# The extra block of a graph network's quantile layer: 16-bit words collected on ScalarE, trees for both neighbours apart, candidates in halves

## The chip, the cores and the metric

The kernel runs on one core of a Trainium2 chip. The metric is the time of one execution on the device in microseconds (us). Engines are named as in the profile: PE is TensorE, PEld its weight load, DVE is VectorE, ACT is ScalarE, POOL is GpSimd, SP is SyncE, which only issues transfers.

## The reference

Four graph layers in sequence over 16 graphs of 1024 nodes with 64 channels; each layer is `x = x + layer(relu(layernorm(x)), adj)`. Only layer 0 bears on the change. For each node it takes the neighbours that are left after a rule has dropped some, sorts their values in each channel, and mixes three quantiles:

```python
vals = jnp.where(nd[..., None], x[:, None, :, :], jnp.inf)
s = jnp.sort(vals, axis=2)
nv = nd.sum(2)
for tau, w in zip((0.25, 0.5, 0.75), (0.25, 0.5, 0.25)):
    pos = tau * jnp.maximum(nv - 1, 0)
    lo, hi = floor(pos), ceil(pos)
    agg = agg + w * (v_lo + (pos - lo) * (v_hi - v_lo))   # entries lo and hi of s
y = relu((x + agg) @ W1 + b1) @ W2 + b2
```

Layers 1 to 3 multiply by the adjacency, with gates, with a small MLP, and with a softmax of attention.

## The kernel before

The 16 graphs are worked on in eight pairs. For a pair, all 1024 values of every channel are sorted once (`sort_pair`); the sorted order is cut into words of 11 values. A product of the neighbour matrix with codes of rank (`wt`, line 975) gives for each node, channel and word a number that packs how many neighbours lie up to there and which of the word's values are neighbours. From these numbers the wanted place is found by maxima over the words (a tree), the bits are decoded (`places`, 28 small VectorE operations), and the value is picked from candidates that TensorE forms from signs and a table of the sorted values (`pick`: five predicated copies; `add_to`: the weighted sum).

`select` does this for one graph in groups of two row tiles of 128 nodes, with windows: only those words are looked at in which a quantile normally lies. Nodes whose quantile lies outside its window are flagged. At the end of `select`, before the values of its last group, `compact` collects the flagged nodes of the graph, at most 64: it gathers their rows of the neighbour matrix and makes all 56 words for them, in seven pieces of eight words (`PIECES`, 512 columns each; line 1288 multiplies, line 1292 evicts), and writes them to DRAM (`x_d`). Graph 0 of the pair has partitions 0 to 63, graph 1 has 64 to 127. It also writes a selection table (`sel_d`) that takes the results back to the nodes.

After both graphs `extras` handles the collected nodes of the pair, 128 rows at once and all words: it loads `x_d` (line 1308), clears and loads the two tables `tab` (lines 1312, 1314), and for each of the three quantiles k evicts the words as 16-bit integers with the quantile's place as a bias (line 1326), transposes them (1333), takes two signs (1336, for the lower and the upper neighbour of the quantile), adds 2048 for the upper neighbour (1340) and runs the tree over both at once (1004 and 1008, in `maxima`), with two outputs z and odd (1346, 1347). Then `places` for all six, and six times: 64 small products into one candidate tile of four PSUM banks (1357), five predicated copies (1065) and the weighted sum (1072, 1074). Last, for each graph of the pair, the selection table is loaded (1365), multiplied (1368) and the flagged nodes of `agg` are overwritten (1369).

Then come the four layers of both graphs (`layers`), which need `agg`. Beside `extras` and `layers`, in the first seven pairs, run the next pair's `neighbours` (scan of line 879, squares of 908 and 909, blocks of 929; transposed copies of the adjacency, lines 885 to 888, which ScalarE evicts and writes out) and the rest of its sort (lines 804 to 814); the forward half of the sort (772 to 776) also runs beside `select`. The last pair has no next one.

The order of instructions on each engine is not the order of the text: a planner orders them by estimated costs, earlier text first among those ready. Each engine then works through its own list in that order. Buffers are tiles of pools; with one buffer of a name, the next tile of that name waits for the last reader of the one before. The memory of `extras` (pool `xs`) is that of `select` before and of `layers` after.

Of the kernel before, what the change touches and what calls it, by code (L numbers as in the profile page):

```python
# [14 lines left out]
I16 = mybir.dt.int16  # L15
# [27 lines left out]
def gnn_stack(ctx, tc, x, adj, nodemask, w, out):  # L43
# [25 lines left out]
    ones_b = const.tile([P, N], BF16, name="ones_b")  # L69
# [92 lines left out]
    x_d = dram.tile([P, NW * C], F32, name="x_d")  # L162
# [292 lines left out]
    def general(gw):  # L455
# [47 lines left out]
        with tc.For_i(0, B, 1) as b:  # L503
            with ExitStack() as per_batch:
# [13 lines left out]
                with (  # L518
# [5 lines left out]
                    notrem = nb1.tile([P, NT, N], BF16, name="notrem")  # L524
                    for t in range(NT):
# [11 lines left out]
                        nc.vector.tensor_tensor_scan(cum, ones_b, ni, 0.0, op0=ALU.mult, op1=ALU.add)  # L537
# [522 lines left out]
    def pick(cand, masks):  # L1060

        v = cand.rearrange("p q (d l) -> p q d l", l=24)
        for (dst, frm, n), mk in zip(PICKS, masks):
            mk = mk.rearrange("p (q d o) -> p q d o", d=4, o=1)
            nc.vector.copy_predicated(
                v[:, :, :, dst : dst + n], mk.to_broadcast([P, NQ, 4, n]), v[:, :, :, frm : frm + n]
            )
        return v[:, :, :, 11]
# [158 lines left out]
    def compact(b, i, wt, row10, out_of, kept, cp, cpp):  # L1227
# [40 lines left out]
        nc.scalar.copy(vx[mine, :], pv[mine, :9])  # L1268
        rows = cp.tile([P, N], F8, name="rows")
# [11 lines left out]
        for u in range(0, len(PIECES), 2):  # L1281
            two = PIECES[u : u + 2]
            n = len(two) * 512
            xr = cp.tile([P, 1024], F32, name="xr")
            for e, g in enumerate(two):
                pw = bank()
                for j in range(NT):
                    nc.tensor.matmul(  # L1288
                        pw, ndx[:, j, :], wt[g][:, j].rearrange("p w c -> p (w c)"),
                        start=(j == 0), stop=(j == NT - 1),  # L1290
                    )
                nc.scalar.copy(xr[mine, e * 512 : (e + 1) * 512], pw[mine])
            nc.sync.dma_start(x_d[mine, two[0] * 512 : two[0] * 512 + n], xr[mine, :n])
# [8 lines left out]
    def extras(pr, kept, aggs, xs, xp):  # L1302

        vx = kept["vx"]
        comb = xs.tile([P, NW * C], F32, name="comb_x")
        for u in range(0, len(PIECES), 2):
            at = slice(PIECES[u] * 512, (PIECES[u] + len(PIECES[u : u + 2])) * 512)
            nc.scalar.dma_start(comb[:, at], x_d[:, at])
        tabs = []
        for i in range(2):  # L1310
            tab = xs.tile([4 * NH, NQ, 4, 48], F16, name=f"tab{i}")
            nc.vector.memset(tab, 0.0)
# [6 lines left out]
        qx = xs.tile([P, 3], F32, name="qx")  # L1319
        nc.vector.tensor_scalar(qx, vx[:, :3], -2048.0, -2048.0, op0=ALU.mult, op1=ALU.add)  # L1320
        signs = []
        z = xs.tile([P, 1, 6, C], U16, name="z_x")
        odd = xs.tile([P, 1, 6, C], U16, name="odd_x")
        for k in range(3):
            y = xs.tile([P, 2, 2 * NQ, 4 * NH], I16, name="y_x", bufs=2)
            nc.scalar.activation(
                y[:, 0].rearrange("p r (h d) -> p r h d", d=4),
                comb.rearrange("p (h r d) -> p r h d", r=2 * NQ, d=4),
                AF.Identity, bias=qx[:, k : k + 1], scale=1.0,
            )  # L1330
            pt = xp.tile([P, 2, 512], F32, name="tr").bitcast(BF16).rearrange("p e (q n) -> p (e q) n", n=P)
            for q in range(NQ):
                nc.tensor.transpose(pt[: 4 * NH, q, :], y[:, 0, q, :].bitcast(BF16), ident_b)
# [6 lines left out]
            nc.vector.tensor_scalar_add(y[:, 1], y[:, 0], 2048.0)  # L1340
            yu = y.bitcast(U16)
            maxima(yu, NH)
            ev, od = yu[:, :, :NQ, :4], yu[:, :, NQ:, :4]
            zs = z[:, 0, 2 * k : 2 * k + 2, :].rearrange("p s (q d) -> p s q d", d=4)
# [373 lines left out]
```

## Time and profile before

| what | value |
|---|---|
| median of 3 runs | 5775.26 us (5774.35 to 5782.18) |
| profiled execution, own time | 5786.15 us |
| its span | 5784.4 us |
| busy: DVE / PE / ACT / PEld / POOL | 5034.9 / 4378.1 / 3789.4 / 2731.3 / 169.8 us |
| transfers | 551.45 MB, 519811 packets, mean 95 GB/s |
| collection's products, L1288 | 896, 379 ns each (median) |
| collection's copies, L1292 | 112, 580 ns each |
| extra block's evictions, L1326 | 24, 3281 ns each (median) |
| candidates' products, L1357 | 3072, 281 ns each (median) |
| first pair: extra block / layers | 684 to 792 / 792 to 982 us |
| last pair: extra block / layers | 5542 to 5619 / 5619 to 5784 us |

The busy times are of one profiled execution. A product's 281 ns is its length in a pipeline: 64 of them take 2.79 us in the last pair. In the same way ScalarE's and VectorE's instructions overlap a little with the one behind; a row of "743.4, 712" means that the group kept the engine busy 743.4 us in all and that one instruction lasted 712 ns.

### The profile page before, as it was taken

To read this page: it belongs to the slowest core of one execution; us is meant where nothing else is said; L and a number is where in the kernel's file an instruction comes from. 1 tells how busy PE (TensorE), PEld (TensorE's weight loads), DVE (VectorE), ACT (ScalarE), POOL (GpSimd) and SP (SyncE) were. 2 spreads that over 40 slices of the span, in tenths; PEclk is the share of its full clock that TensorE was granted. 3 is DMA by queue.
4 is the path that set the end of the run, shared out by engine and by line. 5 is a ranking of instruction groups with operands and counts; after the bars stand their busy time and mean duration, and the time that the engine had idled before them with its cause. 6 is when DMAs were issued, how large, how long until landed. Compare 5 with 4: busy or idle time off the path is not lost.

```text
span 5784.4 us, 114212 instructions
## 1 busy us (share of the span) xinstructions
PE 4378.1 (76%) x45010; PEld 2731.3 (47%) x45010; DVE 5034.9 (87%) x13175; ACT 3789.4 (66%) x5739; POOL 169.8 (3%) x292
## 2 busy tenths in 40 slices
PE   1488677896878958788588885788767886779956
PEld 1355443554435544455434554355543554535642
DVE  9899888998889987999879998899888998888755
ACT  2587657775586855867558666686657866477835
POOL 3000000000000000000000000000000000000000
PEclk5699878997789977899688996899878997789967
DMA  3401264013631047210562115611255012630030
GB/s 128 127 23 45 86 205 133 29 38 113 220 96 35 28 133 237 62 40 23 166 211 55 41 53 167 203 32 40 82 175 172 26 40 90 215 110 18 10 100 5
DMA packets 519811, 551.45 MB, mean 95 GB/s; under 512 B 263296, under 2 KB 413056, under 8 KB 519264
## 3 DMA queue, kind: packets, MB, share of 16 engines
q1 hardware_dynamic: 376864, 459.65, 25.5%
q10 hardware_dynamic: 140064, 81.84, 4.6%
q8 instruction: 355, 5.82, 0.4%
q0 software_dynamic: 2336, 2.57, 0.2%
q14 instruction: 192, 1.57, 0.1%
HBM read 360.17 MB, written 183.76 MB: 94 GB/s over the span
## 4 chain that ended last, share of the span: by engine, by line
PE 40%; DVE 24%; ACT 23%; DMA 9%; issue 3%; POOL 0%; SPq 0%; ACTq 0%; DVEq 0%; POOLq 0%
PE comb L1097 13%; ACT sign L1152 8%; PE cand L1197 6%; PE bank L1462 5%; DVE y L1168 4%; PE comb L1288 3%; ACT y L1105 3%; DMA adjT<-a_d 2%; DVE cum L879 2%; DMA a_d<-at 2%; DVE wt L975 2%; DVE cand L1205 2%; PE pk L929 2%; ACT nat L1128 1%; PE bank L1446 1%
## 5 line engine op out<-in xcount | busy, mean ns | idle before, releaser
L1097 PE MATMUL comb<-wt,ndT 128*128 128x512 fp8e5 x6144 | 1439.2, 386 | 144.4 <-ACT sign L1152 111.8
L1105 ACT ACTIVATE y<-comb,qb 128x512 int16<-128x512 f32 x1152 | 743.4, 712 | 505.3 <-PE comb L1097 504.2
L1097 PEld LDWEIGHTS <-ndT 128*128 128x128 fp8e5 x6144 | 591.1, 99 | 864.7 <-issue 231.6
L1152 ACT ACTIVATE sign<-comb,lower 128x1024 fp8e5<-128x1024 int16 (+1 forms) x640 | 694.5, 1085 | 0.0
L1152 ACT ACTIVATE sign<-comb,half 128x1024 fp8e5<-128x1024 int16 (+1 forms) x640 | 689.1, 1077 | 0.0
L1197 PE MATMUL cand<-vtab,sign 128*128 128x48 f16 (+1 forms) x18432 | 663.1, 191 | 23.1 <-DVE agg L1074 16.2
L1168 DVE TENSOR_TENSOR y<-y 128x512 uint16<-128x512 uint16 (+5 forms) x896 | 669.4, 789 | 10.8 <-PE comb L1150 10.0
L1197 PEld LDWEIGHTS <-sign 128*128 128x128 fp8e5 x18432 | 637.6, 96 | 82.0 <-issue 21.2
L1205 DVE COPY_PREDICATED cand<-w_f,cand 128x256 f32<-128x256 uint16 (+1 forms) x1536 | 531.9, 378 | 86.1 <-PE cand L1197 83.7
L887 ACT COPY at<-pk 128x512 f32<-128x512 f32 x256 | 147.3, 586 | 372.7 <-PE pk L885 199.8
L1150 PE MATMUL comb<-ident_b,y 128*128 128x128 bf16 x4608 | 307.2, 218 | 101.9 <-ACT sign L1152 70.8
L929 PE MATMUL pk<-minus_b,rem 128*128 128x128 bf16 x1024 | 231.9, 251 | 178.8 <-ACT rem L910 178.8
L1150 PEld LDWEIGHTS <-y 128*128 128x128 bf16 x4608 | 284.9, 97 | 127.1 <-issue 126.9
L929 PE MATMUL pk<-ident_b,ni 128*128 128x128 bf16 x1024 | 229.1, 247 | 110.4 <-ACT ndT L935 60.7
L879 DVE TENSOR_TENSOR_SCAN cum<-ni 128x1024 f16<-128x1024 fp8e5 x128 | 292.4, 2285 | 15.5 <-POOL ni L875 15.5
L885 PE MATMUL pk<-ident,a 128*128 128x128 f32 x1024 | 192.1, 330 | 149.9 <-DMA a<-in_adj_dram 100.1
L1462 PE MATMUL bank<-att,hs 128*64 128x512 f32 x512 | 191.1, 857 | 122.0 <-ACT hs L1578 122.0
L1462 PE MATMUL bank<-adjT,nd 128*64 128x512 f32 x896 | 256.2, 642 | 29.9 <-DMA adjT<-a_d 29.6
L975 DVE TENSOR_SCALAR wt<-node 128x2048 uint8<-128x2048 f16 x224 | 262.5, 1220 | 18.4 <-PE comb L1288 18.1
L775 DVE TENSOR_TENSOR s<-s 128x512 f32<-128x512 f32 (+1 forms) x440 | 276.0, 627 | 0.0
L776 DVE TENSOR_TENSOR s<-s 128x512 f32<-128x512 f32 (+1 forms) x440 | 275.1, 625 | 0.0
L1163 DVE TENSOR_SCALAR y<-y 128x4608 int16<-128x4608 int16 x128 | 173.5, 1355 | 90.7 <-ACT y L1105 89.3
(381 smaller groups left out, 8355.7 us busy)
## 6 DMA issues: line engine op xcount, KB each, us to landing
adjT<-a_d SPq DMA_DIRECT2D x336, 512.0 KB
a<-in_adj_dram SPq DMA_DIRECT2D x128, 512.0 KB
a_d<-at ACTq DMA_DIRECT2D x256, 256.0 KB
m_d<-swapped SPq DMA_DIRECT2D x104, 512.0 KB
swapped<-m_d SPq DMA_DIRECT2D x104, 512.0 KB
n_d<-nat SPq DMA_DIRECT2D x128, 128.0 KB
x_d<-xr SPq DMA_DIRECT2D x48, 256.0 KB
comb_x<-x_d ACTq DMA_DIRECT2D x24, 512.0 KB
```

The source lines that it names most:

```text
L775: nc.vector.tensor_tensor(to_lo, lo, hi, op=ALU.max)
L879: nc.vector.tensor_tensor_scan(cum[:, t - t0, :], ni[:, t, :], wide[:, t, pad - 1 : pad - 1 + N], 0.0, op0=ALU.add, op1=ALU.add)
L929: nc.tensor.matmul(pk[:, n % 4, :], lhs, rhs, start=(n % 4 == 0 and m == 0), stop=(m == len(terms) - 1 and last),)
L975: nc.vector.tensor_scalar(wt[g][:, :, k : k + 4, :].bitcast(U8), node, 4.0 * (25 + CODE * (8 * g + k)), 4.0 * 26, op0=ALU.add, op1=ALU.min,)
L1097: nc.tensor.matmul(pw, ndT[:, j, t * P : (t + 1) * P], wt[1 + g8][:, j].rearrange("p w c -> p (w c)"), start=(j == 0), stop=(j == NT - 1),)
L1105: nc.scalar.activation(y[:, 0, chunks, at : at + 8 * d_].rearrange("p q (w d) -> p q w d", d=d_), pw.rearrange("p (w q d) -> p q w d", w=8 ...
L1150: nc.tensor.transpose(pt[:, q - q0, :], y[:, 0, q, :].bitcast(BF16), ident_b)
L1152: nc.scalar.activation(signs[tl][s][:, q0:q1, :], pt.bitcast(I16), AF.Sign, bias=before[s], scale=-1.0, saturate=False,)
L1168: nc.vector.tensor_tensor(v[:, :, :, :n], v[:, :, :, :n], v[:, :, :, n : 2 * n], op=ALU.max)
L1197: nc.tensor.matmul(cand[:, e, at : at + 12 * d_].rearrange("p (d l) -> p d l", l=12), signs[tl][sec][:, chunk, :], tab[:, q, :, half_ * 12 ...
L1205: nc.vector.copy_predicated(v[:, :, :, dst : dst + k], mk.to_broadcast([P, 2, C // 2, k]), v[:, :, :, frm : frm + k])
L1462: nc.tensor.matmul(po[to : to + C, :], lhs, rhs[:, f * HALF : (f + 1) * HALF], start=(j == 0), stop=(j == NT - 1))
```

## The change

The words of the collected nodes no longer go to DRAM as 32-bit numbers and through ScalarE again in `extras`. `compact` evicts each piece three times, once for each quantile's bias, as 16-bit integers, into a tile with two buffers, and writes each piece to DRAM by itself. An eviction writes its output in order and reads the product in steps of four columns. `extras` loads the 16-bit words of all three quantiles with 12 transfers into one tile `y_x` with room for both neighbours, and transposes from it with words 32 elements apart.

The tables are cleared by GpSimd. One addition makes the upper neighbour's words of all three quantiles; the trees run once for the upper and once for the lower neighbour, over all three quantiles at a time, first over the pieces and then inside a piece. The upper neighbour's tree does not touch the words that the transposes read. The candidates come in halves of 8 chunks, in three tiles of two PSUM banks that the transposes and the last products use too. Both selection tables are loaded at once, from ScalarE's queue, into the memory of `y_x` when the trees are done with it. A constant of ones is made smaller to leave room; the general path that it served (not run here) gets its own.

```diff
-    x_d = dram.tile([P, NW * C], F32, name="x_d")
+    x_d = dram.tile([P, 7, 3, 512], I16, name="x_d")
...
     compact:
+        qx = cp.tile([P, 3], F32, name="qx")
+        nc.vector.tensor_scalar(qx[mine], pv[mine, :3], -2048.0, -2048.0, op0=ALU.mult, op1=ALU.add)
...
-        for u in range(0, len(PIECES), 2):
-            two = PIECES[u : u + 2]
-            xr = cp.tile([P, 1024], F32, name="xr")
...
-                nc.scalar.copy(xr[mine, e * 512 : (e + 1) * 512], pw[mine])
-            nc.sync.dma_start(x_d[mine, two[0] * 512 : two[0] * 512 + n], xr[mine, :n])
+        for g in PIECES:
+            xr = cp.tile([P, 3, 512], I16, name="xr", bufs=2)
+            pw = bank()
...
+            for k in range(3):
+                nc.scalar.activation(
+                    xr[mine, k].rearrange("p (h d r) -> p h d r", h=4, d=4),
+                    pw[mine].rearrange("p (h r d) -> p h d r", r=2 * NQ, d=4),
+                    AF.Identity, bias=qx[mine, k : k + 1], scale=1.0,
+                )
+            nc.sync.dma_start(x_d[mine, g], xr[mine])
...
     extras:
-        comb = xs.tile([P, NW * C], F32, name="comb_x")
-            nc.scalar.dma_start(comb[:, at], x_d[:, at])
+        y = xs.tile([P, 2, 3, 7, 512], I16, name="y_x")
+        for g in (1, 3, 5, 0):
+            for k in range(3):
+                here = slice(g, g + (2 if g else 1))
+                nc.scalar.dma_start(y[:, 0, k, here], x_d[:, here, k])
...
-            nc.vector.memset(tab, 0.0)
+            nc.gpsimd.memset(tab, 0.0)
...
         for k in range(3):
-            y = xs.tile([P, 2, 2 * NQ, 4 * NH], I16, name="y_x", bufs=2)
-            nc.scalar.activation(
-                y[:, 0].rearrange("p r (h d) -> p r h d", d=4),
-                comb.rearrange("p (h r d) -> p r h d", r=2 * NQ, d=4),
-                AF.Identity, bias=qx[:, k : k + 1], scale=1.0,
-            )
-            pt = xp.tile([P, 2, 512], F32, name="tr")
+            pt = xp.tile([P, 1024], F32, name="two", bufs=3)
+            by_word = y[:, 0, k].rearrange("p g (w r) -> p r (g w)", w=16)
             for q in range(NQ):
-                nc.tensor.transpose(pt[: 4 * NH, q, :], y[:, 0, q, :].bitcast(BF16), ident_b)
+                nc.tensor.transpose(pt[: 4 * NH, q, :], by_word[:, q].bitcast(BF16), ident_b)
...
-            nc.vector.tensor_scalar_add(y[:, 1], y[:, 0], 2048.0)
-            maxima(yu, NH)
+        nc.vector.tensor_scalar_add(y[:, 1], y[:, 0], 2048.0)
+        for s in (1, 0):
+            yu = y[:, s].bitcast(U16)
+            for n, m in ((3, 4), (2, 2), (1, 1)):
+                nc.vector.tensor_tensor(yu[:, :, :n], yu[:, :, :n], yu[:, :, m : m + n], op=ALU.max)
+            yw = yu[:, :, 0]
+            for n in (256, 128):
+                nc.vector.tensor_tensor(yw[..., :n], yw[..., :n], yw[..., n : 2 * n], op=ALU.max)
...
+        sel_t = xs.tile([P, 2, 3, 7, 512], I16, name="y_x")
+        for i in range(2):
+            nc.scalar.dma_start(sel_t[:, i], sel_d[i])
...
         for s in range(6):
-            cand = xp.tile([P, NQ, P], F32, name="cand")
-            for q in range(NQ):
+            for q0 in range(0, NQ, 8):
+                cand = xp.tile([P, 1024], F32, name="two", bufs=3)
+                for q in range(8):
...
-            v = pick(cand[:, :, :96], [mk[:, 0, s, :] for mk in (odd, *marks)])
+                here = slice(q0 * 4, (q0 + 8) * 4)
+                v = pick(cand[:, :, :96], [mk[:, 0, s, here] for mk in (odd, *marks)])
...
         for i in range(2):
-            sel_t = xs.tile([P, NT, P], F32, name="sel_t")
-            nc.sync.dma_start(sel_t, sel_d[i])
-            ps = xp.tile([P, 2, 512], F32, name="tr")
+            ps = xp.tile([P, 1024], F32, name="two", bufs=3)
```

## The prediction

> **What bounds the kernel now.** I read the page's busy times first, then its chain, then the windows of one pair and of the last pair, the chain of waits in the last pair's extra block, and the rows of the lines that change.
>
> ```profile
> span 5784.4 us, 114212 instructions
> PE 4378.1 (76%) x45010; PEld 2731.3 (47%) x45010; DVE 5034.9 (87%) x13175; ACT 3789.4 (66%) x5739; POOL 169.8 (3%) x292
> PE 40%; DVE 24%; ACT 23%; DMA 9%; issue 3%; POOL 0%; SPq 0%; ACTq 0%; DVEq 0%; POOLq 0%
> ```
>
> VectorE is the fullest engine, but the chain that ends last is on PE more often: the kernel is a relay of stages, and a stage must be read by itself. In the windows (PE, PEld, DVE, ACT, POOL busy, then granted clock, DMA share and GB/s):
>
> ```profile
> 684.00:700.00 16.00, 1.19 (x10) 0.92 (x10) 9.97 (x20) 4.25 (x2) 1.76 (x4) 0.50 0.82 246
> 684.00:792.00 108.00, 53.65 (x784) 46.31 (x784) 97.09 (x232) 68.46 (x86) 7.01 (x12) 0.67 0.50 153
> 792.00:982.00 190.00, 149.05 (x735) 70.92 (x735) 153.29 (x467) 119.98 (x168) 4.67 (x9) 0.79 0.61 194
> 5542.00:5612.00 70.00, 26.35 (x448) 24.56 (x448) 42.80 (x94) 21.10 (x9) 0.32 (x2) 0.50 0.33 117
> 5619.00:5784.00 165.00, 112.27 (x407) 50.65 (x407) 82.04 (x269) 79.08 (x107) 2.88 (x4) 0.72 0.02 4
> ```
>
> 684 to 792 is the first pair's extra block, 792 to 982 its four layers; the last two rows are the same two stages of the last pair, where nothing of a next pair runs beside them. In the first seven pairs the block is nearly full on VectorE (97 of 108 us), but only some 47 us of that is its own: the rest is the next pair's sort and neighbours. In the last pair the block is bare (42.8 of 70 us), and its chain shows what it waits for:
>
> ```profile
> 5542.38 1.34 DVE tab L1312
> 5543.99 1.34 DVE tab L1312
> 5545.38 3.29 ACT y_x L1326
> ...
> 5579.52 2.79 PE cand L1357 x64
> 5582.33 0.97 DVE cand L1065
> ...
> 5585.18 2.79 PE cand L1357 x35
> ```
>
> TensorE fills the one candidate tile for 2.79 us while VectorE waits; VectorE picks from it for some 2.85 us while TensorE waits; six times over. The order of the chain before that is memsets, an eviction of 3.29 us, transposes, tree.
>
> **The extra block, cost by cost (per pair).** Off ScalarE: three evictions of 3.28 us, 9.8 us. Off VectorE: two memsets of 1.34 us, 2.7 us; they go to GpSimd. The nearest row there is the memset of 128x2048 16-bit words, 1.80 us; 3072 words are then 2.7 us, or 1.35 us if counted as 1536 words of 32 bits. Behind them on GpSimd wait the diagonal products L875, which VectorE's scans need; they come some 5 us apart here, so I take nothing. The tables they clear are loaded by 8 issues (6.7 us) and needed more than 20 us after the values end, which hides both; without that cover it is 5 us.
>
> Trees: before, per word k, L1008's rows: 3584 elements 2.02 us, 256 elements 0.285 us, so 0.152 us and 0.52 ns an element. Per k: 2.02 + 1.09 + 0.29 + 0.55 + 2 x 0.28 + 2 x 0.22 = 4.95; three 14.9 us. After, per neighbour: 4608, 3072, 1536, 768, 384 elements are 2.55 + 1.75 + 0.95 + 0.55 + 0.35, and two outputs of 192, written in steps of 4, at 0.25 to 0.35: 6.75 us; two 13.5 us. The three additions of 1.09 become one of 3.0 us.
>
> Picks: copies of 768, 256 and 64 take 0.956, 0.421 and 0.222 us: 0.153 us each and 1.045 ns an element. A whole candidate is 0.956 + 2 x 0.421 + 0.29 + 0.22 + 0.28 = 2.59 us; a half is 0.55 + 2 x 0.29 + 0.22 + 0.19 + 0.24 = 1.78 us. Twelve halves are 21.4 us against 15.5, +5.9 us. VectorE in all: -2.7 - 0.3 - 1.4 + 5.9 = +1.5 us a pair.
>
> On the path in the last pair: before, from the end of the values (5542.1) to the end of the first selection product (5611.7) 69.6 us. After: addition 3.0, trees 13.5, places 7.2 (8.3 from 5570.9 to 5579.2, less 1.1 of picks between), twelve halves 21.4 (TensorE needs 1.4 a half, less than 1.78, and has three tiles), product 3.7: 48.8 us, 20.8 less. The transposes (48 x 0.12 = 5.9 us) run under the first tree, which touches only the other half of the words; the six signs (11.7 us) end before the picks. The last pair's block has to be loaded by 5542: the last piece was written out from 5532.7, and the old load was issued by 5537.4. The new one has 12 issues for 4, at the old median of 0.59 us, 4.7 us more on ScalarE's queue. I take 3 us of that: **-18 us** for the last pair (-10 to -22).
>
> The loads carry 128 x 3584 x 6 bytes, 2.75 MB for 1.84, in runs of 1 KB; at the 246 GB/s of the first row, 3.7 us later. On ScalarE's queue they wait for the last piece's write, and behind them stand the next pair's copies L887 and their write-outs; before, the loads were issued after several of these (at 684.5, the last piece's write at 670.0), so there is room, and I take nothing. In the first seven pairs the chain gains the same 20.8, less 2.7 of memsets that were hidden there behind a late load, less 3.7; and a wait of 4.9 us goes:
>
> ```profile
> 781.44 2.01 PE tr L1368 x16
> 783.45 0.02 issue
> 783.47 4.88 DMA sel_t<-sel_d
> 788.35 0.14 issue
> 788.48 3.66 PE tr L1368 x16
> ```
>
> The second selection table had one buffer and was loaded only after the first product, 4.9 us; now both are loaded once the trees are done, from ScalarE's queue. If the trees end later than the planner thought, neighbours' squares and copies stand behind these two issues; that is within the range. 20.8 - 2.7 - 3.7 + 4.9 = 19.3; I let the layers start 18 us earlier. Not all of it stays: about 18 us of the next pair's sort and neighbours that filled the block must now run beside the layers, where VectorE goes from 153 to 171 of 190 us. The layers alone take 165 us (last row). I take half, **9.5 us a pair, -66 us** for seven. Ends: all 18 (-126), or nothing.
>
> **The collection (16 times).** Seven copies of 0.58 us become 21 evictions; L1105, the same size and output with a bias, has
>
> ```profile
> L1105 ACT ACTIVATE y<-comb,qb 128x512 int16<-128x512 f32 x1152 | 743.4, 712 | 505.3 <-PE comb L1097 504.2
> L1292 ACT COPY xr<-comb 64x512 f32<-64x512 f32 x112 | 61.9, 580 | 199.6 <-DMA x_d<-xr 131.6 <-PE comb L1288 68.0
> ```
>
> 743.4 / 1152 = 0.645 us when packed, so 13.5 us for 4.1. A piece is 1.94 us of ScalarE beside 8 products of TensorE, 13.3 to 14.8 / 7 = 1.9 to 2.1 us. The old waits for the write-out (48 of them, 131.6 / 48 = 2.7 us, in a round trip of 3.05 us) came every second piece. With two buffers a third piece waits for the first: two pieces take 1.94 + 3.05, so seven take 3 x 4.99 + 1.94 = 16.9 us, against 14.2 measured from the first copy to the end of the last. That is +2.7 us if all of it is on the path, and nothing where the last group's candidates cover it on TensorE. I take 1.5: **+24 us** (0 to 43). SyncE issues 7 writes for 4.
>
> Two new strides have no row. The evictions read PSUM with a step of 16 bytes, the transposes load words 64 bytes apart. L1326 read steps of 4 words in SBUF at 3281 / 3584 = 0.92 ns an element, dense speed; L1105 read runs of 4. I take the dense price. At double, an eviction is about 1.07 us (its 0.43 us of elements twice), and the loads 5.9 us more under the first tree.
> [...]
>
> **Sum.** -18 - 66 + 24 = -60 us on the profiled execution's own 5786.15 us (span 5784.4). That run is 10.9 us above the median, so against 5775.26 it is **5715 us**.
>
> **Rivals.**
> *Collection paced by ScalarE (slower).* Evictions at 1.07 us make a piece 3.2 us and a collection 22.5 us, +8 of 14.2: 16 x 8 = +128, with the gains of 84 left, 5775 + 44 = 5819. It decides from 0.93 us an eviction (16 x (21 x 0.93 - 14.2) = 84). For it: the unseen stride, and ScalarE's 505 us of waiting at L1105 that shows TensorE normally ahead. Against: L1326's price. The write-out alone, with nothing gained in the seven pairs, gives +25.
> *VectorE as the bound: no change.* The block was 90% full; the saved time returns in the layers and the next selection, whose windows VectorE fills to 94% (182 of 194 us). Then -18 and some +18: 5775. That the planner puts other work between the halves, so that they do not overlap, ends here too.
> *All stays.* The layers' windows have 37 us of idle VectorE, more than the 18 displaced: -126 - 22 + 10 = 5637.
>
> **How the numbers follow.** Forecast 0.45, all stays 0.18, no change 0.15, collection 0.22. The range runs from all gains without cost, 5775 - 148 = 5627, to the collection's case, less its tail: **5627 to 5812**. A measurement of this kernel tells about 0.2% (12 us) from no change. Faster: 0.45 x 0.97 + 0.18 + 0.15 x 0.25 = 0.65; slower: 0.22 x 0.95 + 0.15 x 0.25 = 0.25; same 0.10. The forecast's own range is 5680 to 5750.
>
> **What would show it.** The last pair from values to first product near 51 us, with copies of 384 elements near 0.55 us and no PE-VectorE alternation; the first pair's second aggregate copy near 774 if its values end as now; the layers' windows longer by 9 us at 90% VectorE. Evictions near 0.65 us packed, a collection near 16 us. Wrong if an eviction is above 0.93 us, if the loads land more than 10 us later, or if the windows after the block grow by all that it lost.

## The result, and the profile after

The changed kernel takes 5845.99 us (median of 4 runs, 5839.31 to 5863.43) against 5778.72 us for the kernel before on the same chip: ratio 1.0116, 95% interval 1.0101 to 1.0132. It is slower by 67 us; 60 us faster was predicted, and the range ended at 5812.

First the page's head of the profiled execution (5839.31 us): span, busy time of each engine, and the engines' shares of the chain that ended last.

```profile
span 5837.5 us, 114806 instructions
PE 4389.8 (75%) x45010; PEld 2766.2 (47%) x45010; DVE 5089.6 (87%) x13359; ACT 3840.6 (66%) x5939; POOL 226.6 (4%) x308
PE 34%; DVE 34%; ACT 18%; DMA 9%; issue 3%; POOL 1%; SPq 0%; ACTq 0%; DVEq 0%; POOLq 0%
```

The span grew by 53.1 us (from 5784.4), VectorE's busy time by 54.7, so VectorE is idle for 747.9 us, as before (749.5). Its share of the last chain rose from 24% to 34%.

Then the windows of the stages; the columns are those of the prediction. For the first pair: extra block (end of the collection to the second graph's aggregate), rest of the stage up to the next pair's first weights, both together; then the last pair's block, and the last pair whole.

```profile
661.80:755.74 93.94, 54.70 (x807) 48.24 (x805) 80.86 (x190) 42.62 (x60) 11.91 (x13) 0.68 0.59 177
755.74:987.30 231.56, 160.01 (x953) 84.16 (x954) 188.91 (x562) 142.38 (x205) 8.53 (x13) 0.78 0.59 185
661.80:987.30 325.50, 214.71 (x1760) 132.39 (x1759) 269.76 (x750) 185.00 (x265) 20.44 (x26) 0.75 0.59 183
5597.30:5669.70 72.40, 38.82 (x689) 36.61 (x687) 48.45 (x145) 16.46 (x15) 0.38 (x2) 0.64 0.56 190
5231.80:5837.50 605.70, 475.69 (x4955) 294.30 (x4954) 420.22 (x1162) 388.02 (x597) 10.54 (x10) 0.86 0.12 35
```

The same five windows of the kernel before, cut at the same events:

```profile
664.40:792.94 128.54, 67.95 (x1045) 58.75 (x1044) 113.46 (x266) 74.79 (x98) 8.25 (x15) 0.71 0.57 174
792.94:976.70 183.76, 143.16 (x711) 67.22 (x709) 147.51 (x462) 117.11 (x164) 4.67 (x9) 0.79 0.60 194
664.40:976.70 312.30, 211.11 (x1754) 125.97 (x1752) 260.97 (x727) 191.90 (x262) 12.93 (x24) 0.76 0.59 186
5528.86:5619.49 90.63, 38.04 (x689) 35.76 (x686) 52.36 (x125) 22.98 (x13) 0.32 (x2) 0.58 0.46 151
5156.50:5784.40 627.90, 480.29 (x4969) 295.41 (x4967) 422.83 (x1150) 385.17 (x578) 5.22 (x8) 0.84 0.11 32
```

The first pair's block became 34.6 us shorter (128.5 to 93.9), the rest of its stage 47.8 us longer (183.8 to 231.6). VectorE's work inside the block fell by 32.6 us (113.46 to 80.86) and grew by 41.4 us in the rest (147.51 to 188.91): besides its own gain the block got shorter because the planner put less of the next pair's work into it. Over the whole stage VectorE is busy 84% before (260.97 of 312.30) and 83% after (269.76 of 325.50). In the last pair, where nothing runs beside, the block is 18.2 us shorter and the whole pair 22.2. So the span's +53.1 is +76.8 in the first seven pairs (11.0 a pair), -22.2 in the last and -1.5 ahead of the first.

The third reading is the chain of the last pair's block (start, duration, what):

```profile
5603.84 4.99 DMA x_d<-xr
5608.89 7.07 DMA tab<-t_d
5615.98 2.10 DMA y_x<-x_d
5618.12 9.39 PE two L1331 x48
5627.54 7.63 DVE y_x L1344 x5
...
5654.29 1.33 DVE two L1067 x6
5655.77 0.93 DVE two L1067 x4
5656.85 1.33 DVE two L1067 x6
5658.39 1.38 PE two L1367 x32
5659.77 2.15 issue
5661.92 7.08 PE two L1378 x32
```

The alternation of 2.79 us of TensorE and 2.85 us of VectorE is gone: in the last five halves TensorE fills one in 0.87 us (the last in 1.36) and VectorE picks from one every 1.15 to 1.42 us. What is new is the start: last piece's write, tables, loads, transposes.

The fourth is the end of the first pair's stage in the chain, where the time of the seven pairs went:

```profile
961.76 2.33 PE pk L931 x20
964.60 1.04 ACT sq L911
965.64 0.76 ACT ndT L937 x2
966.40 1.05 ACT rem L912
967.49 1.46 PE pk L931 x23
968.96 0.84 PE pk L931 x12
970.48 1.75 PE pk L941 x64
975.23 1.06 ACT s L850
976.34 1.13 PE ps L855 x4
978.14 1.13 PE ps L855 x4
979.90 2.91 DMA y_d<-s
982.82 2.54 DMA node<-y_d
985.98 1.13 DVE s L705
987.35 13.72 DVE wt L977 x12
```

All of it is the next pair's work: squares, remainders and blocks of its second graph's neighbours, then the last copies of its sort, then the codes from which the next weights are made. The layers had ended at 951.6. Before, they ended at 980.0, 3 us after the next weights had begun, and no such tail was left. The tail isn't empty: VectorE is busy for 27.9 of its 35.7 us.

### The profile page after: what moved, and what is told of

Same layout as the page of the kernel before. It is cut to its first block, busy times and chain, and to the rows that moved or that the text cites. A ratio compares the mean times of both kernels' runs of the same rounds, so it can differ in the third digit from the quotient of the medians.

```text
span 5837.5 us, 114806 instructions
## 1 busy us (share of the span) xinstructions
PE 4389.8 (75%) x45010; PEld 2766.2 (47%) x45010; DVE 5089.6 (87%) x13359; ACT 3840.6 (66%) x5939; POOL 226.6 (4%) x308
## 4 chain that ended last, share of the span: by engine, by line
PE 34%; DVE 34%; ACT 18%; DMA 9%; issue 3%; POOL 1%; SPq 0%; ACTq 0%; DVEq 0%; POOLq 0%
PE comb L1099 10%; DVE y L1170 6%; ACT sign L1154 5%; PE bank L1472 5%; PE cand L1199 5%; DVE cand L1207 4%; PE pk L931 3%; DMA adjT<-a_d 2%; DVE cum L881 2%; ACT y L1107 2%; DVE wt L977 2%; DVE s L777 2%; DVE s L778 2%; DVE swapped L776 1%; DVE y L1165 1%
## 5 line engine op out<-in xcount | busy, mean ns | idle before, releaser
L931 PE MATMUL pk<-ident_b,ni 128*128 128x128 bf16 x1024 | 241.4, 255 | 204.0 <-ACT at L889 98.9
L931 PE MATMUL pk<-minus_b,rem 128*128 128x128 bf16 x1024 | 243.7, 260 | 198.5 <-ACT rem L912 197.8
L931 PEld LDWEIGHTS <-rem 128*128 128x128 fp8e5 x1024 | 119.9, 117 | 335.0 <-ACT rem L912 251.5
L1294 ACT ACTIVATE xr<-comb,qx 64x512 int16<-64x512 f32 x336 | 201.2, 675 | 95.4 <-DMA x_d<-xr 47.1
```

Of the source, the lines that this page charges most:

```text
L931: nc.tensor.matmul(pk[:, n % 4, :], lhs, rhs, start=(n % 4 == 0 and m == 0), stop=(m == len(terms) - 1 and last),)
```

## The experiments

Times of different sets of runs are compared by their ratio to the kernel before, which ran beside each. In the expectations, "collection's end" is the last product into the flagged rows (line 1289), "next weights" the first instruction of line 977. Five theories are used. 1: a pair ends with the later of the layers and the next pair's work. 2: VectorE's work sets the end. 3: any edit of the order throws the time. 4: the next pair's loads stand behind stores on SyncE's queue. 5: only the next pair's work counts, the layers may run on.

**The halves, undone and alone.** In the changed kernel:

```diff
-            for q0 in range(0, NQ, 8):
-                cand = xp.tile([P, 1024], F32, name="two", bufs=3)
+            cand = xp.tile([P, NQ, P], F32, name="cand")
```

> The changed kernel with its candidates whole again, in one tile of four banks, and the transposes in one tile of two banks; all else as changed. Theory 1 (displaced work): the block got 36 us shorter a pair, and what ends the pair now is the next pair's neighbours and sort, which the planner put behind the layers. A block made some 10 us longer again by the alternation of PE and VectorE then costs nothing much or even gains: 5800 to 5850 us, with the block near 105 us for 95 and the stretch from the block's end to the next weights shorter by 10 us or more. Theory 2 (added work): VectorE has 5 us more a pair, most of it in the halves' copies, and VectorE bounds the pairs; taking the halves away gives back 7 x 5 = 35 us: about 5810 us, with that stretch unchanged.

Measured 5793.07 us, ratio 1.0027 [1.0010, 1.0045]. In the kernel before, the opposite edit:

> The kernel before with the candidates in halves, in three tiles shared with the transposes; all else as before. Both theories say a shorter block in the last pair, by 10 to 12 us. Theory 1: in the other pairs a block that is some 10 us shorter is given back, as the next pair's work moves behind the layers; 5765 to 5800 us. Theory 2: 12 copies more a pair with 5 us more of VectorE cost 7 x 5 = 35, less 12: about 5800 us, without a longer stretch from the layers' end to the next weights.

Measured 5752.74 us, ratio 0.9948 [0.9928, 0.9968]: faster than both kernels. The same edit gives 0.5% to the one and costs the other 0.9%, so it has no price of its own. The blocks, as means of seven pairs from the collection's end, are 130.7 us in the kernel before, 119.6 in the changed one without halves, 107.2 with halves alone and 94.8 in the changed kernel; the next weights come at 313.5, 314.7, 314.9 and 326.1 us. Twenty-three microseconds off the block (130.7 to 107.2) brought the end of the stage no earlier, it came 1.4 us later, and with the next twelve it came later by 11. Of the 31 us that halves alone take off the span, 13.6 come in the last pair, where nothing runs beside.

**The next pair's neighbours ahead of the layers**, in the text from which the planner makes its order, in the changed kernel and in the one before:

```diff
+                made = prepare(pr + 1, nb, nbp)
                 for i, (ly, lb) in enumerate(((ly0, lb0), (ly1, lb1))):
                     layers(pr * 2 + i, (pr * 2 + i) % 4, aggs[i], ly, lb, held[i])
-                made = prepare(pr + 1, nb, nbp)
                 sort_pair(pr + 1, cur, sop)
```

> The changed kernel with the next pair's neighbours written ahead of the layers in the text, so that the planner prefers them; no instruction is added or taken away. Theory 1: the tail of squares, blocks and copies after the layers goes, and the pair ends some 15 to 30 us earlier: 5650 to 5750 us, faster than both kernels. Theory 2: the same work in another order; 5830 to 5860 us.

Measured 5796.68 us, ratio 1.0020 [1.0009, 1.0032]: with the same instructions 0.96% less than the changed kernel. Theory 2 in its plain form falls with that.

> The kernel before with the same edit of the text, as a control for the order alone. Theory 1: there the neighbours end before the layers (967 against 980 us in the first pair), so they don't set the end; preferring them delays the layers: 5770 to 5850 us, no gain. If the order alone is worth as much here as in the changed kernel, the displacement is not what the change brought on.

Measured 5885.91 us, ratio 1.0170 [1.0150, 1.0190]. The order that helps the changed kernel costs the one before 1.7%.

**Doses of the same.** If theory 1 were enough, half doses should give half gains. First the neighbours of one graph ahead of the layers, in the changed kernel and in the kernel before with halves:

```diff
+                made = prepare(pr + 1, nb, nbp, (0,))
                 for i, (ly, lb) in enumerate(((ly0, lb0), (ly1, lb1))):
                     layers(...)
-                made = prepare(pr + 1, nb, nbp)
+                made += prepare(pr + 1, nb, nbp, (1,))
                 sort_pair(pr + 1, cur, sop)
```

> The changed kernel, with the neighbours of the next pair's first graph written ahead of the two graphs' layers and those of its second graph still behind them, as a half dose of the run with both ahead (5796.68 us). No instruction is added or taken away. Theory 1 (a pair ends with the later of two works, the layers and the next pair's neighbours and sort; the change let the layers start early and left the second graph's neighbours for a tail of their own): the layers end some 5 to 10 us later than the 290 us after the collection's end that they take in the changed kernel, the neighbours end 10 to 20 us before their 313 us, and the seven pairs get 5 to 15 us shorter each: 5740 to 5810 us. Theory 2 (VectorE has 5 to 8 us more to do in a pair and sets the end): 5830 to 5850 us, as the changed kernel. Theory 3 (any other order of the text throws the planner's order by tens of microseconds, and the change was such a throw): no forecast, 5750 to 5900 us, and then the ends of layers and neighbours don't tell the time.

> The kernel before with the half candidates alone (5752.74 us), and the neighbours of the next pair's first graph ahead of the layers. Theory 1: there the layers end 298 us and the neighbours 307 us after the collection's end, close to balance, so that a half dose gives at most some 4 us a pair and may cost as much by making the layers late: 5725 to 5800 us, less gain than the same edit brings to the changed kernel. Theory 2: VectorE's work is the same as without the edit, 5745 to 5760 us. Theory 3: anything up to 5880 us.

Measured 5887.52 us (1.0187 [1.0169, 1.0205]) and 5895.71 us (1.0207 [1.0164, 1.0250]): both slower than without the edit. In the first the neighbours did end earlier (308 us after the collection's end for 314) and the layers later (297 for 290), as theory 1 said; but the sort's last step moved from 314 to 322 us, and the next weights came at 333.5. Then layers and neighbours in turns, and the sort alone ahead:

```diff
                 for i, (ly, lb) in enumerate(((ly0, lb0), (ly1, lb1))):
                     layers(...)
+                    made = (made if i else []) + prepare(pr + 1, nb, nbp, (i,))
-                made = prepare(pr + 1, nb, nbp)
                 sort_pair(pr + 1, cur, sop)
```

> The changed kernel with the text in turns: layers of the first graph, neighbours of the next pair's first graph, layers of the second graph, neighbours of the next pair's second graph, sort. No instruction is added or taken away. Theory 1: a smaller dose than the neighbours of one graph ahead of both layers: the first graph's layers end as in the changed kernel, the second graph's later, the neighbours earlier; 5760 to 5835 us. Theory 2: 5830 to 5850 us. Theory 3: no order among the three doses.

```diff
+                sort_pair(pr + 1, cur, sop)
                 for i, (ly, lb) in enumerate(((ly0, lb0), (ly1, lb1))):
                     layers(...)
                 made = prepare(pr + 1, nb, nbp)
-                sort_pair(pr + 1, cur, sop)
```

> The changed kernel with the text of the next pair's sort ahead of the layers and that of both graphs' neighbours still behind them. No instruction is added or taken away. Theory 1, with the neighbours as the late end: the sort's last stores no longer stand at 310 us after the collection's end, but the neighbours' second half still ends behind the layers; at most the 3 to 10 us between the neighbours' end and the next weights are saved: 5770 to 5850 us, and not less than with one graph's neighbours ahead. If instead the sort is the late end, 7 to 12 us a pair are saved and this run is the fastest of the doses: 5750 to 5790 us. Theory 2: 5830 to 5850 us.

Measured 5917.37 us (1.0232 [1.0213, 1.0252]) and 6145.22 us (1.0630 [1.0610, 1.0649]). With the sort ahead its last step started at 204 us, the layers ended at 310, the neighbours at 375: a bare tail of 65 us. There is no ordered dose; which of three works comes last depends on the order, and something always does. None of these eight times lies in the range that theory 1 or theory 2 had given for it; a range of theory 3, which names no cause, held once (5887.52 us). The leave-out runs below, not these, carry the argument.

**Left out: the next pair's neighbours**, in the kernel before and in the changed one:

```diff
-                made = prepare(pr + 1, nb, nbp)
...
-                layers(pr * 2 + i, (pr * 2 + i) % 4, ...)
+                layers(pr * 2 + i, i, ...)
```

> The kernel before, leaving out the neighbours of the second to the eighth pair: every pair uses the lists and the transposed rows that the first pair made, so its outputs are not the reference's. Block, layers, sort and selection stay whole. It is the base for the next run. Theory 1 (the pair ends with the later of layers and next pair's work): the stage from the collection's end to the next weights, 313 us before, falls to 265 to 290 us; 5480 to 5630 us in all. Theory 2 (VectorE's work sets the stage): 58 us of VectorE less a pair, 250 to 260 us, 5350 to 5420 us in all.

> The changed kernel, leaving out the neighbours of the second to the eighth pair in the same way; its outputs are not the reference's. Theory 1: with the late end gone, the shorter block (95 us for 131) shows in the pair's end: 15 to 30 us a pair and 20 us in the last pair faster than the run before it, 125 to 230 us in all. Theory 2: VectorE has 5 to 8 us more to do a pair: slower by 15 to 40 us, the last pair's 20 us already counted. Theory 3 (the planner's order is thrown by any edit): no forecast.

Measured 5591.37 and 5526.66 us: the changed kernel is 65 us faster, where it is 67 us slower with the neighbours. The sign is theory 1's, the size (125 to 230) is not. In the second run the sort's last step starts at 270 us, 3 us after the layers' end; in the first it started at 172. So a second work was still put behind the layers. The next weights even come later in the second run (281.8 us for 273.0): its gain stands in the selection behind them, 377.4 us for 393.5, where in the first run the layers ran on 21 us into it.

**One queue.** In the first pair of the changed kernel SyncE's queue waited for the last layer's results, with the next pair's loads behind them (line, what it waited for, us in total, times, longest):

```profile
SPq L1598 <- DVE nd L1596: 18.8, 2, 12.1
```

The loads of the neighbours' rows and the stores of the result were moved to GpSimd's queue, in both kernels:

```diff
-                nc.sync.dma_start(a, adj[b, t * P : (t + 1) * P, :])
+                nc.gpsimd.dma_start(a, adj[b, t * P : (t + 1) * P, :])
...
-            nc.sync.dma_start(by_half(out[b]...
+            nc.gpsimd.dma_start(by_half(out[b]...
```

> The changed kernel, with the loads of the neighbours' rows and the stores of the result issued from GpSimd and no longer from SyncE. Nothing else is changed. In the first pair of the changed kernel SyncE's queue waited 18.8 us for the last layer's results, to store them, with the next pair's loads for sort and neighbours behind them; before, the last of those loads had gone out 50 us earlier. Theory 4 (the tail is a matter of one queue in order: the planner put the next pair's loads behind the stores): the neighbours of the second graph and the sort end 10 to 20 us earlier, 5700 to 5790 us. Theory 2: 5830 to 5850 us. Theory 1 in its bare form, with the work itself late on VectorE and ScalarE and the loads only following it: 5820 to 5850 us.

> The kernel before, with the same two kinds of transfers issued from GpSimd: the control. Theory 4: its loads did not stand behind the stores, so it gains little: 5750 to 5800 us. Theory 3 (any edit throws the order): up to 100 us in either direction.

Measured 5829.59 us (1.0087 [1.0056, 1.0119]) and 5799.37 us (1.0036 [1.0022, 1.0050]). The first is 0.3% less than the changed kernel, with intervals that overlap, and the neighbours still end at 314 us. Theory 4 falls as the main cause.

**Left out: everything of the next pair.** Besides the neighbours the sort goes too, and what was read by pair is read from the first one:

```diff
-                    sort_pair(pr + 1, cur, sop)
-                if pr + 2 < pairs:
-                    cur = sort_begin(pr + 2, sop)
...
-        nc.sync.dma_start(node[:, :, 0, :], y_d[b])
+        nc.sync.dma_start(node[:, :, 0, :], y_d[b % 2])
```

> The kernel before, leaving out both the neighbours and the sort of the second to the eighth pair: every pair uses what was made for the first one, so its outputs are not the reference's. Selection, block and layers stay whole and have nothing beside them. It is the base for the next run. From the last pair, where this is so in the kernel before: block 91 us, layers 159, selection and collection some 370, 620 a pair and some 5270 us in all.

> The changed kernel, leaving out the neighbours and the sort of the second to the eighth pair in the same way; its outputs are not the reference's. Theory 1 (the seven pairs' gain was lost to the next pair's work): every pair now gains what the last one did, 18 us, 8 x 18 = 144 us less than the run before it (110 to 160). Theory 2 (the change itself costs elsewhere, in the collection, the selection or the layers): clearly less, under 100 us.

Measured 5328.00 and 5171.86 us: 156 us, 19.5 a pair. This decides whether the gain is lost beside the next pair's work or the change costs elsewhere: it is lost beside that work. The collection, the selection and the layers cost nothing new (from the first weights to the last collection's end 395.5 us for 395.3, from the second aggregate to the layers' end 180.4 for 179.7); alone, every pair gains what the prediction had worked out for the block. The busy times of the two pages, first without the change and then with it, show VectorE at 67 and 70%, far from full:

```profile
PE 3962.6 (74%) x40306; PEld 2402.8 (45%) x40306; DVE 3596.7 (67%) x9696; ACT 3123.9 (59%) x4703; POOL 92.7 (2%) x152
```

```profile
PE 3953.4 (77%) x40306; PEld 2401.8 (46%) x40306; DVE 3604.6 (70%) x9880; ACT 3180.5 (62%) x4903; POOL 135.9 (3%) x168
```

From the spans and VectorE's busy times of the three pairs of runs:

| beside block and layers | span, change | VectorE busy, change | VectorE idle: before, after |
|---|---|---|---|
| nothing | 5329.1 to 5167.3, -161.8 | +7.9 | 1732.4, 1562.7 |
| sort | 5585.7 to 5515.4, -70.3 | +20.3 | 855.4, 764.8 |
| sort and neighbours | 5784.4 to 5837.5, +53.1 | +54.7 | 749.5, 747.9 |

The change takes 170 us of waiting out of VectorE's day when there is nothing else to do, and next to nothing when the waits were full of the next pair's work.

**The next pair ahead of all layers, and between them:**

```diff
+                made = prepare(pr + 1, nb, nbp)
+                sort_pair(pr + 1, cur, sop)
                 for i, (ly, lb) in enumerate(((ly0, lb0), (ly1, lb1))):
                     layers(...)
-                made = prepare(pr + 1, nb, nbp)
-                sort_pair(pr + 1, cur, sop)
```

> The changed kernel with both the neighbours and the sort of the next pair written ahead of the layers. No instruction is added or taken away. In every kernel so far in which something of the next pair stood behind the layers in the text, its end came last. Theory 5 (what the next selection needs is the next pair's work alone, the layers can run on into it): the next weights come at 285 to 305 us after the collection's end for 326, the layers end 20 to 50 us after them and make the first selection 15 to 25 us longer: 5700 to 5800 us. Theory 1 (the later of the ends counts, the layers' too): 5800 to 5900 us, because the layers then end some 30 us later than anything else. Theory 2: 5830 to 5850 us.

```diff
                     layers(...)
+                    if i == 0:
+                        made = prepare(pr + 1, nb, nbp)
+                        sort_pair(pr + 1, cur, sop)
```

> The changed kernel with the neighbours and the sort of the next pair written between the first graph's layers and the second graph's. No instruction is added or taken away. Theory 5: the second graph's layers are the ones that run on into the next selection, the first graph's end early: 5700 to 5800 us, next weights at 290 to 310 us after the collection's end. Theory 1: as the run before it or somewhat better, since the work behind is half as long: 5780 to 5850 us. Theory 3 (any edit of the order throws it by up to 100 us, with no order among them): up to 5930 us.

Measured 5926.69 us (1.0248 [1.0228, 1.0267]) and 5925.43 us (1.0227 [1.0201, 1.0252]). Theory 5 falls on its price: the next weights came at 258 and 280 us, earlier than it said, and the layers ran on; but the first selection beside them (first weights to the second graph's) took 261 and 243 us for 180, not 15 to 25 more. What leaves the stage is paid in the selection.

**The tables' memsets back on VectorE:**

```diff
-            nc.gpsimd.memset(tab, 0.0)
+            nc.vector.memset(tab, 0.0)
```

> The changed kernel with the two memsets of the tables back on VectorE. In the changed kernel VectorE is busy 54.7 us longer than before and idle for the same 748 us, so that its added work is the whole loss. One instruction in a pair there, the comparison of the neighbours' rows, took 2.92 us each of the seven times that it started beside GpSimd's memset, and 0.68 us otherwise. If GpSimd's memset holds VectorE up, this kernel has no comparison above 1 us, and VectorE's busy time is only 21 - 7 x 2.2 = 6 us higher. If VectorE's busy time sets the kernel's (theory 2): 5840 to 5865 us, slightly slower. If the order of work does: anything from 5780 to 5880 us, and then idle time changes by more than busy time.

Measured 5782.54 us, ratio 0.9990 [0.9972, 1.0008]: undoing this one line takes 1.26% off the changed kernel, as much as its whole loss. Line 876 (minimum, median and maximum in ns), in the changed kernel and in this one:

```profile
L876 DVE TENSOR_SCALAR ni<-a x128: 639/680/2917, 52.8 to 5183.2; 128x1024 fp8e5<-128x1024 f32 x128
```

```profile
L876 DVE TENSOR_SCALAR ni<-a x128: 625/684/702, 53.0 to 5134.8; 128x1024 fp8e5<-128x1024 f32 x128
```

The hold-up is real, and gone: 7 x 2.2 = 15 us. In the last pair of the changed kernel one step of the decoding (line 1024) stood as well, 5.79 us for 0.28. The rest isn't explained by it. VectorE's busy time fell by 20.6 us (5089.6 to 5069.0) where 6 more were expected, and its idle time by 33.7; the block is 88.6 us for 94.8, and the next weights come at 319.7 us for 326.1. A second hold-up it is not: no other line's durations fell by more than 3.0 us in all, and the durations of all VectorE instructions added up are even longer (6058.9 us for 6026.5). Busy time counts overlaps once, and more instructions overlap the one behind in this run, whose order differs.

**Additions and trees by word again:**

```diff
-        for s in (1, 0):
-            yu = y[:, s].bitcast(U16)
+        for k in range(3):
+            nc.vector.tensor_scalar_add(y[:, 1, k], y[:, 0, k], 2048.0)
+            yu = y[:, :, k].bitcast(U16)
```

> The changed kernel with additions and trees again by word, both neighbours in one instruction (the same halvings, three additions and three trees, 3 x 4.95 us by the rows of the kernel before). 16-bit words, half candidates and both selection tables stay. It parts what still lies between the kernel before with halves (5752.74 us) and the changed one. Theory 2: VectorE's busy time changes by under 5 us in all, so 5835 to 5860 us, and idle time stays near 748 us. Theory 1 with the planner's order: the trees of the first word can start before the last load has landed, the block is up to 5 us shorter alone, and the time is anything between 5750 and 5860 us, idle time changing with it.

Measured 5824.32 us, ratio 1.0051 [1.0032, 1.0071]: 0.65% less than the changed kernel, though the block is longer (100.3 us for 94.8). VectorE's busy time is 8.5 us more (5098.1), its idle time 23 less (724.6).

## Why the prediction was wrong

**The step that failed** is "I take half, **9.5 us a pair, -66 us** for seven". The layers did start earlier, by 36 us and not 18, and not half but more than all was handed back: +77 us, 11.0 a pair. The prediction had the mechanism in hand ("about 18 us of the next pair's sort and neighbours that filled the block must now run beside the layers"), and its own sign of being wrong came true, "the windows after the block grow by all that it lost" (47.8 us for 34.6). Its rival "VectorE as the bound: no change" was the nearest.

As means of the seven pairs, the stretch from the collection's end to the next weights grew by 12.6 us; in it VectorE is busy 8.8 us longer and idle 3.8 us longer, and the selection behind it is 2.5 us shorter. So the shorter block brought back no idle time of VectorE, and the added work came on top. Of the 8.8 us the records trace 5: halves 5.8, line 876 beside the memsets 2.2, less 2.7 for the memsets that left VectorE. In the kernel before with halves the same stretch has as much added work (8.9 us) but 7.5 us less idle time, and grew by only 1.4.

What both lacked is that the stage ends with three works, layers, neighbours and sort, on engines that each follow a fixed list. Taking idle time from one does not shorten the stage if that idle time was where the others ran: alone the change gives 156 us, beside the sort 65, beside sort and neighbours it costs 67. Which work then lies bare at the end is set by the order: here the next pair's second graph, 36 us from the layers' end to the next weights. The ceiling "All stays", with "37 us of idle VectorE" in the layers' windows, failed, as we read it, for the same reason: idle time inside a stage is room only if the work that could fill it is next on its engine's list. That reading is argued; no run tests it by itself.

**A cost taken at nothing.** Of the memsets' move the prediction said that the diagonal products wait behind them on GpSimd, "so I take nothing", and it counted 2.7 us of VectorE as gained. It did not ask whether VectorE itself would stand. It did, for 15 us in the first seven pairs and 5.5 in the last: 21 us, as much as the sixteen memsets had cost on VectorE (16 x 1.34). Undoing the move gave 1.26%, the most of the three parts that were undone; how that comes about beyond the 21 us, with the order or through the loads of the tables, stays open.

**The last pair was right, in part by luck**: -18 us predicted, -18.2 measured in the block and -22.2 in the pair. By the prediction's own measure, from the end of the values to the end of the first selection product, it is 54.8 us for 69.6, so -14.8 ("near 51" was said); 3.7 us came with the second product, which ends 3.4 us after the first and no longer 7.1, a gain that had been counted for the first seven pairs only. The terms erred in both directions. The words landed later than the 3 us taken: VectorE waited 8.99 us for them from the end of the values, in the chain behind a write of 4.99 us and behind 7.07 us of the table loads that the prediction had called hidden. The 48 transposes took 9.39 us, not 5.9, so that the second tree waited 2.4 on the mean. Two outputs of 192 elements in steps of four took 0.60 and 0.62 us, twice the price taken. Against that the decoding and the picks interleave: from the last output to the last sum 23 us, where the sum had 7.2 + 21.4, made of durations that overlap by some 0.1 us each.

**The collection was wrong by all of its +24 us**, to the good side. The rows of the changed kernel (line, engine, operation, tiles, count; busy, mean ns; idle before):

```profile
L1294 ACT ACTIVATE xr<-comb,qx 64x512 int16<-64x512 f32 x336 | 201.2, 675 | 95.4 <-DMA x_d<-xr 47.1 <-PE comb L1289 47.1 <-PE comb L1304 0.8
L1331 PEld LDWEIGHTS <-y_x 128*112 128x112 bf16 x384 | 73.6, 283 | 110.4 <-DMA y_x<-x_d 52.8 <-issue 42.9 <-DMA tab<-t_d 14.7
```

201.2 / 336 = 0.599 us a packed eviction, under the 0.645 taken; the wait for the write-out is 47.1 us in all, for 131.6 before. From the first eviction to the end of the last a collection takes 16.6 us for 15.1 before (means of 16; the 14.2 of the prediction is the first one's), which is the 1.5 us that it had taken. But they were not on the path: the collection's products take 13.7 us for 13.9, and from the second graph's weights to its last product 199.3 us pass for 199.6. The rival in which the collection paces the time is out.

Of the two strides, ScalarE's reads in steps of four columns show no cost against the eviction that reads runs of four, 0.599 us for 0.645; the double price in the rival's 1.07 us was the author's estimate and is shown by no run. The plain copy of the same 64 x 512 before, with another output and no bias, took 61.9 / 112 = 0.553, so a small cost is not excluded. TensorE's weight loads of words 64 bytes apart took longer: a load lasts 283 ns (median) against 217 for the dense ones before, and from one load's start to the next 190 ns pass against 107. In the last pair the granted clock was 0.50 under both.

**VectorE's work.** Halves cost 5.8 us a pair in records (the copies 36.3, the sums 10.0 us over eight pairs), 5.9 predicted; the trees gain 0.1 us and not 1.4. Net the page shows 54.7 us more, 6.8 a pair, where 1.5 had been taken; the 21 us of standing beside the memsets are in it. It is not the cause by itself: the kernel before with halves has 50.3 us more (5085.2), and is 0.5% faster.

**What stays open** is why the planner's order falls as it does for each edit. Small edits that add no instruction moved the time by 0.3 to 5%, in opposite directions for the two kernels, and the three undone parts (halves 0.9%, memsets 1.26%, trees 0.65%) add up to 2.8%, more than twice the loss. They can't be read as prices, the 1.26% of the memsets' line included. That the gain is lost in the overlap with the next pair is shown; no single one of the orders tried brought it back.

## What to carry to other kernels

Before costing a shorter path, ask who was using its idle time: where a next stage's work fills it, the gain of the bare path (read from a stage where nothing runs beside) was not reached here (19.5 us a pair alone, a loss of 11.0 beside the next pair's work), and the fullest engine's share of the whole stage up to the next dependency, 84% here before and 83% after, told more. Take one-line parts of a change apart before believing the whole: here the halves alone beat both kernels (5752.74 us), and undoing one line that moved a memset to an idle engine took off as much as the change had lost. GpSimd, 3% busy before, was not free here: beside its memsets an instruction of VectorE, 87% busy, took 2.92 us for 0.68, once in each of seven pairs.

## What the runs showed of the hardware

In the changed kernel line 876 on VectorE started seven times while GpSimd cleared the two tables (5.25 us for both); each time it took 2.92 us for 0.68 and ended 0.55 us after the second memset. Alone, with nothing of a next pair, one of the decoding's steps met the tables' memsets (2.7 us each) instead of line 876:

```profile
L1024 DVE TENSOR_SCALAR w_m<-z x64: 293/293/6035, 323.5 to 4908.4; 128x512 uint16<-128x512 uint16 x64
```

It took up to 6.0 us for 0.29, somewhat longer than both memsets together (5.4 us). In the changed kernel itself one such step, in the last pair, took 5.79 us. Predicated copies (0.22 and 0.29 us), weighted sums (0.26 to 0.28) and a scan (2.28) that ran beside the same memsets in the changed kernel kept their usual times. Why some instructions stood and others did not is not shown. By its record the step of 6.0 us began 0.6 us ahead of the first memset and stood all the same; no run here explains that.
